# Transfers issued by SyncE stay in traced order through all eight batches of the first feed-forward, and the second feed-forward's preparation yields once more before its transposes

## The chip, the cores and the metric

The kernel runs on one core of a Trainium2 chip. The metric is the device time of one execution in microseconds (us). Before the change three runs took 2148.97, 2151.57 and 2152.36 us: the median is 2151.57. The engines are called by the profile's names: PE (TensorE matmuls), PEld (its weight loads), DVE (VectorE), ACT (ScalarE), POOL (GpSimd) and SP (SyncE, which here only issues transfers). A name with a q (SPq, ACTq) is the engine's own instruction queue as it issues transfers.

## The reference

x has 8 sequences of 512 tokens with 512 features. Two layers follow each other, and each adds two gated branches to x. Everything is float32.

```python
x = x + tanh(g_xattn[0]) * L0_xattn(layernorm(x), ctx)     # gated linear attention, 16 heads
x = x + tanh(g_ffn[0])   * L0_ffn(layernorm(x))            # 512 -> 2048, GELU, 2048 -> 512
x = x + tanh(g_xattn[1]) * L1_xattn(layernorm(x), ctx)     # softmax over 64 context rows
x = x + tanh(g_ffn[1])   * L1_ffn(layernorm(x))            # routed experts

# L0_ffn
h = gelu(x @ proj1.T + proj1_bias);  out = h @ proj2.T + proj2_bias

# L1_ffn: 8 of 32 experts, each 512 -> 2*192 -> 512
probs = softmax(x @ gate_weight.T);  top 8, normalised;  w_tg = sum of them by group
gu, dn = gate_up_proj[dominant_experts], down_proj[dominant_experts]
gate, up = split(x @ gu);  out = sum over g of w_tg * ((silu(gate) * up) @ dn)
```

## The kernel before

**Stages.** The work goes by batch (one sequence) through three stages: "xa0" (the first attention) for all eight batches, then "ff0" (the first feed-forward), then "ff1" (second attention and routed feed-forward together). In `work_list` the entries 0 to 7 are xa0, 8 to 15 are ff0 and 16 to 23 are ff1, so `n` in the main loop (L1365) is 8 to 15 in the first feed-forward and 16 to 23 in the second. Between stages x lies in DRAM: `load_x` (L142) brings a batch's 1 MB in on SP, `store_x` (L162) sends it out on ACT's queue (L170) after ff0, and on SP to the output after ff1.

**Products.** Every product is done by a scheme with seven half-size products (`ORDER`, L703) in place of eight. One step of the main loop is one of the seven: for an up product 8 matmuls with 128 x 256 outputs (L752), for ff0's down product 32 (L868), for ff1's down product 42 (L939), where the scheme is applied twice. The results are gathered in a few PSUM banks and combined by ACT copies (L764) and DVE additions (L807, L884). An ff0 batch has 35 steps (the first 33), an ff1 batch 49 or 50. The last two (or one) products of a unit are put behind the first of the next unit (`steps`, L1121), so a batch's x is complete at its successor's third step. Its store is traced at step 6 (`flush`, L1395).

**Weights.** They stream from DRAM through a ring of 16 tiles of 256 KB (`RING`, L129). After each step as many loads are traced as the step has freed tiles (L1379): one for an up product, four for an ff0 down product. So loads run 16 tiles ahead. They are issued on SP (L1292, L1300).

**The builder.** The weight combinations of the second feed-forward are made while the first one runs: `build_weights("ff1", ...)` (L347) loads raw expert weights on SP (L329, L340), combines them on POOL (`combining`, L232, and L388) and stores them in DRAM on SP (L366, L391). It is a generator, advanced once every fourth step (`next(builder)`, L1399). Its two buffers (`buildp`) take turns, so a load waits for the stores of the chunk before the last one. For each of the six up chunks one advance traces the next chunk's load and the first combination, three trace the others, and one traces seven stores of 256 KB. For each of the three down chunks one traces the load, eight trace a POOL operation each, and one traces seven stores of 448 KB. Its 61 advances fit in the eight batches.

**Preparation.** While batch n runs, batch n+1 is prepared by a generator (`prep_ff0`, `prep_ff1`) that the main loop advances now and then: `steps_of` (L1360) says how many advances there are and L1415 spreads them evenly over the batch's steps less six. `prep_ff1` first does the cross attention (`cross_attention`, L552), then `normed(..., "ff1_b")` (L395), the router, and the shares of the routed groups, which go to DRAM and come back spread over partitions (`spread_share`, L687, on SP). In `normed` DVE takes the statistics of x's four token tiles (L404, L405), adds epsilon (L409), POOL raises to the power -1/2 (L411), DVE normalises a tile (L418, `norm`), TensorE transposes it (L425) and ACT copies the transpose out (L428; both in `turn`). For the ff1 call there is one yield between the statistics and the first `norm` and `turn` (L412). x for batch n+2 is loaded at step 20 (L1404).

**Order.** The tile framework schedules the traced instructions: it may move an instruction ahead of others on its engine when its own model says that it is ready sooner. The wrapper `Ordered` (L47) gives an instruction an edge to the one traced before it on its engine, so that it stays behind everything traced earlier there. It does so for the engines that are in the set `in_order` at that moment. Such an instruction shows the wrapper's line, L60, in the profile, and a freely scheduled one its own line. During the attention stage the set holds "sync" and, in places, others. At L1341 it is reduced to "sync". In the main loop it is cleared at the start of every batch after the first of ff0, and `cross_attention` clears it too, after it has kept one DVE copy in order:

```python
        if n != at:
            if n > B:
                in_order.clear()
```

Of the kernel before, what the change touches and what calls it, by code (L numbers as in the profile page):

```python
# [31 lines left out]
B, S, D = 8, 512, 512  # L32
# [36 lines left out]
def flamingo_kernel(  # L69
# [23 lines left out]
    in_order = {"tensor", "vector", "scalar", "gpsimd", "sync"}  # L93
# [15 lines left out]
    def psum(name):  # L109
        return bank["ps"].tile([P, 512], F32, tag="ps", name=name)  # L110
# [284 lines left out]
    def normed(ph, b, tag):  # L395

        xb = xs[ph, b]
        xnT = work.tile([P, NC, S], F32, tag="xnT", name=f"xnT_{tag}")
        mv = small.tile([P, NT, 2], F32, tag="mv", name=f"mv_{tag}")
        if ph == "xa0":  # L400
            in_order.add("vector")
        for t in range(NT):
            st = small.tile([P, 6], F32, tag="st", name=f"st_{tag}_{t}")
            nc.vector.bn_stats(st, xb[:, t, :])  # L404
            nc.vector.bn_aggr(mv[:, t, :], st)  # L405
        if b:
            in_order.discard("vector")
        var = small.tile([P, NT], F32, tag="var", name=f"var_{tag}")
        nc.vector.tensor_scalar(var, mv[:, :, 1], LN_EPS, None, ALU.add)  # L409
        rstd = small.tile([P, NT], F32, tag="rstd", name=f"rstd_{tag}")  # L410
        nc.gpsimd.tensor_tensor(rstd, var, neg_half, ALU.pow)  # L411
        if ph == "xa0" or tag.startswith("ff1") or tag == "ff0_0":  # L412
            yield
        xn = {}

        def norm(t):
            xn[t] = work.tile([P, D], F32, tag="xn", name=f"xn_{tag}_{t}")
            nc.vector.tensor_scalar(  # L418
                xn[t], xb[:, t, :], mv[:, t, 0:1], rstd[:, t : t + 1], ALU.subtract, ALU.mult
            )  # L420

        def turn(t):
            pt = psum(f"pt_{tag}_{t}").rearrange("p (c q) -> p c q", q=P)
            for c in range(NC):
                nc.tensor.transpose(pt[:, c, :], xn[t][:, ts(c, P)], ident)  # L425

            at = t % 2 * 2 + t // 2 if tag.startswith("ff1") else t
            nc.scalar.copy(xnT[:, :, ts(at, P)], pt)  # L428

        if ph == "xa0" and b == 0:  # L430
            norm(0)
            norm(1)
            yield
            for t in range(NT):
                turn(t)
                if t + 2 < NT:
                    norm(t + 2)
                yield
            return xnT
        for t in range(NT):  # L440
            norm(t)
            turn(t)
            yield
        return xnT
# [82 lines left out]
    def prep_xa0(b):  # L527
        xnT = yield from normed("xa0", b, f"xa0_{b}")
        yield "last"
        blocks["xa0", b] = xnT, token_combinations("xa0", b, xnT)  # L530
# [12 lines left out]
    def prep_ff0(b):  # L543
        xnT = yield from normed("ff0", b, f"ff0_{b}")

        xb = xs["ff0", b]
        for t in range(NT):
            nc.gpsimd.tensor_tensor(xb[:, t, :], xb[:, t, :], b2_sb, ALU.add)  # L548
        yield "last"
        blocks["ff0", b] = xnT, token_combinations("ff0", b, xnT)  # L550

    def cross_attention(b):  # L552

        xb = xs["ff1", b]
        c2 = hpool.tile([P, D], F32, tag="ctx", name=f"ctxd_{b}", bufs=2)
        for h in range(2):
            nc.gpsimd.dma_start(out=c2[ts(h, M), :], in_=ctx_in[ts(b, M), :])
        maskf = small.tile([P, M], F32, tag="maskf", name=f"maskf_{b}")
        in_order.add("vector")
        nc.vector.tensor_copy(maskf, mask_sb[:, ts(b, M)])  # L560
        in_order.clear()
        shift = small.tile([P, M], F32, tag="shift", name=f"shift_{b}")
        nc.vector.tensor_scalar(shift, maskf, 1.0, NEG, ALU.subtract, ALU.mult)
        gate = small.tile([P, 1], F32, tag="gate", name=f"gate_{b}")
        nc.vector.reduce_max(gate, maskf, AX.X)
        nc.vector.tensor_scalar(gate, gate, gate_xa1, None, ALU.mult)
        ctxT = hpool.tile([P, NC, M], F32, tag="ctxdT", name=f"ctxdT_{b}", bufs=2)
        nc.gpsimd.dma_start(out=ctxT, in_=turned[b])
        xnT = yield from normed("ff1", b, f"xa1_{b}")

        pst = psum(f"pst_{b}")[:, 0:H2]
        for c in range(NC):
            for r in range(2):
                nc.tensor.matmul(  # L576
                    pst[ts(r, M), :],
                    lhsT=ctxT[:, c, :],
                    rhs=xnT[:, c, :].rearrange("p (u r q) -> p r u q", u=2, r=2)[:, r],
                    start=c == 0,  # L580
                    stop=c == NC - 1,
                )
        scT = hpool.tile([P, H2], F32, tag="scT", name=f"scT_{b}", bufs=1)
        nc.scalar.copy(scT, pst)
        yield
        psc = psum(f"psc_{b}")[:, 0:H2]
        for u in range(2):
            nc.tensor.transpose(psc[:, ts(u, P)], scT[:, ts(u, P)], ident)
        psc = psc.rearrange("p (t m) -> p t m", m=M)
        sc = hpool.tile([P, NT, M], F32, tag="sc", name=f"sc_{b}", bufs=1)  # L590
        nc.vector.scalar_tensor_tensor(
            sc, psc, 1.0 / math.sqrt(D), maskf.unsqueeze(1).to_broadcast([P, NT, M]), ALU.mult, ALU.mult
        )
        nc.vector.tensor_tensor(sc, sc, shift.unsqueeze(1).to_broadcast([P, NT, M]), ALU.add)
        top = small.tile([P, NT], F32, tag="top", name=f"top_{b}")
        nc.vector.tensor_reduce(top, sc, AX.X, ALU.max, negate=True)
        yield
        total = small.tile([P, NT], F32, tag="total", name=f"total_{b}")
        for t in range(NT):
            nc.scalar.activation(  # L600
                sc[:, t, :], sc[:, t, :], AF.Exp, bias=top[:, t : t + 1], accum_out=total[:, t : t + 1]
            )
        coef = small.tile([P, NT], F32, tag="coef", name=f"coef_{b}")
        nc.vector.reciprocal(coef, total)
        nc.vector.tensor_scalar(coef, coef, gate, None, ALU.mult)
        yield
        pe = psum(f"pe_{b}")[:, 0 : 2 * P].rearrange("p (u q) -> p u q", q=P)
        for u in range(NT // 2):
            nc.tensor.transpose(
                pe[:, u, :], sc[:, ts(u, 2), :].rearrange("p t m -> p (t m)"), ident  # L610
            )
        eT = hpool.tile([P, NT // 2, P], F32, tag="eT", name=f"eT_{b}", bufs=1)
        nc.scalar.copy(eT, pe)
        yield
        for t in range(NT):
            pr = psum(f"pr_{b}_{t}")
            half = ts(t % 2, M)
            nc.tensor.matmul(pr, lhsT=eT[half, t // 2, :], rhs=c2[half, :], start=True, stop=True)  # L618
            nc.vector.scalar_tensor_tensor(
                xb[:, t, :], pr, coef[:, t : t + 1], xb[:, t, :], ALU.mult, ALU.add  # L620
            )
            if t % 2:
                yield

    def prep_ff1(b):
        yield from cross_attention(b)
        xnT = yield from normed("ff1", b, f"ff1_{b}")

# [374 lines left out]
    class QUp(Up):  # L1003
        ph, i = "xa0", 0
# [354 lines left out]

    def steps_of(ph, b, _):  # L1360

        return 5 if ph == "ff0" else 21 if b else 23

    at, held = None, False
    for u, m, n in plan:  # L1365
        if n != at:
            if n > B:
                in_order.clear()
            if at is not None and n < 3 * B:
                for _ in work_list[n][2]:  # L1370
                    pass
            at, k, held = n, 0, False
# [39 lines left out]

        until = sum(p == n for _, _, p in plan) - 6
        count = steps_of(*work_list[n + 1])
        if k * count // until > (k - 1) * count // until:  # L1415
            held = next(prep, None) == "last"
# [47 lines left out]
```

## Time and profile before

The profiled execution took 2147.87 us, with a span of 2146.1 us from its first to its last instruction, and a mean granted TensorE clock of 0.995 of full speed. The table takes stretches of the span that lie inside the stages (all times in us; the busy time of PE counts matmuls).

| stretch | what runs | length | PE busy | DVE busy | POOL busy | DMA share | clock |
|---|---|---|---|---|---|---|---|
| 0 to 50 | loads, keys and values | 50.00 | 41.71 | 16.06 | 14.10 | 0.78 | 0.93 |
| 200 to 250 | first attention | 50.00 | 50.00 | 40.96 | 11.54 | 0.51 | 1.00 |
| 401.9 to 501.3 | first feed-forward, batch one | 99.40 | 99.40 | 32.18 | 34.14 | 0.95 | 1.00 |
| 501.3 to 601.5 | batch two | 100.20 | 98.63 | 33.15 | 38.09 | 0.77 | 1.00 |
| 601.5 to 717.3 | batch three | 115.80 | 101.20 | 34.26 | 20.58 | 0.71 | 0.96 |
| 717.3 to 815.8 | batch four | 98.50 | 98.50 | 30.24 | 6.05 | 0.54 | 1.00 |
| 1111.8 to 1220 | batch eight, prepares ff1 | 108.20 | 107.49 | 42.41 | 7.52 | 0.55 | 1.00 |
| 1650 to 1700 | second feed-forward | 50.00 | 49.98 | 39.80 | 0.00 | 0.89 | 1.00 |

A line of the timeline has the start, the duration, the engine, the source line, the operation, what it writes and reads, the shape and the count. In brackets at the end stands how long the engine was idle before it and what ended that idle time: "[11.40 <-ACT u_ff L764]" says that it stood 11.40 us until ACT's instruction at L764 that writes u_ff was done. A transfer's duration on SPq or ACTq is that of its issue, not of the transfer.

### The profile page before, as it was taken

The numbers are of one execution on the slowest core, as the hardware profiler recorded it, in microseconds if no ns is written. First come the engines' busy times: TensorE is split into PE (matmuls) and PEld (weight loads), VectorE is DVE, ScalarE is ACT, GpSimd is POOL, SyncE is SP. The second block draws the span as 40 slices with busy tenths as digits, with TensorE's granted clock in tenths as the row PEclk, the third lists the DMA queues.
The fourth block names the chain that finished last, engine by engine and source line by source line (L and its number), as shares of the span: only waits on it lengthen the run. The fifth ranks groups of instructions, "written<-read, shape, count | busy, mean of one in ns | idle before, by whom it ended". The sixth has DMA issues, their size and how long they took to land.

```text
span 2146.1 us, 30885 instructions
## 1 busy us (share of the span) xinstructions
PE 2094.4 (98%) x11452; PEld 1807.5 (84%) x11452; DVE 1242.7 (58%) x2289; ACT 557.0 (26%) x1146; POOL 251.0 (12%) x228
## 2 busy tenths in 40 slices
PE   8999999999979999999999999999999999999998
PEld 4778887788868888888888889898988989898988
DVE  3687787533323323232426278777767777776857
ACT  3433332212112213030314131222222221312121
POOL 3131111332340001010001000000001010000000
PEclk9999999999999999999999999999999999999999
DMA  7345634799686555555555558677676858585865
GB/s 224 116 153 176 201 109 125 222 316 333 209 260 206 188 151 187 153 186 172 167 184 158 192 168 270 199 247 221 213 247 191 271 164 287 161 282 161 268 202 165
DMA packets 258453, 434.84 MB, mean 203 GB/s; under 512 B 34304, under 2 KB 75936, under 8 KB 254208
## 3 DMA queue, kind: packets, MB, share of 16 engines
q1 hardware_dynamic: 250864, 406.10, 60.0%
q10 hardware_dynamic: 5856, 23.20, 3.0%
q0 software_dynamic: 1584, 3.57, 0.6%
q8 instruction: 92, 1.51, 0.3%
q14 instruction: 57, 0.47, 0.1%
HBM read 369.00 MB, written 63.77 MB: 202 GB/s over the span
## 4 chain that ended last, share of the span: by engine, by line
PE 79%; issue 8%; DVE 6%; DMA 4%; POOL 2%; SPq 1%; ACT 1%; ACTq 0%; POOLq 0%; DVEq 0%
PE x_ff L752 24%; PE w_ff L752 12%; PE x_ff_down L868 10%; PE z_ff L752 6%; PE x_ff_down L939 5%; PE w_ff_down L868 5%; PE w_ff_down L939 3%; PE z_ff_down L868 3%; PE z_ff_down L939 2%; PE v_ff_down L939 2%; PE pt_ff L425 1%; PE pt_xa L425 1%; PE pr L618 1%; PE pst L576 1%; DMA x_ff<-x_ff 1%
## 5 line engine op out<-in xcount | busy, mean ns | idle before, releaser
L764 ACT COPY u_ff<-x_ff 128x512 f32<-128x512 f32 x240 | 140.0, 584 | 758.5 <-PE x_ff L752 728.9
L752 PE MATMUL x_ff<-S_ff,w_ff_up 128*128 128x256 f32 x1280 | 306.1, 382 | 14.8 <-ACT u_ff L764 14.8
L752 PE MATMUL w_ff<-S_ff,w_ff_up 128*128 128x256 f32 x1280 | 304.5, 380 | 0.6 <-DVE a_ff L807 0.6
L752 PE MATMUL x_ff<-xnT_ff,w_ff_up 128*128 128x256 f32 x1280 | 296.8, 380 | 0.8 <-ACT u_ff L764 0.8
L752 PEld LDWEIGHTS x_ff<-S_ff,w_ff_up 128*128 128x128 f32 x1280 | 239.7, 191 | 53.4 <-ACT u_ff L764 15.8
L752 PEld LDWEIGHTS x_ff<-xnT_ff,w_ff_up 128*128 128x128 f32 x1280 | 238.9, 190 | 38.1 <-ACT u_ff L764 6.0
L752 PEld LDWEIGHTS w_ff<-S_ff,w_ff_up 128*128 128x128 f32 x1280 | 240.6, 190 | 35.5 <-issue 3.1
L868 PE MATMUL x_ff_down<-w_ff_down,a_ff 128*128 128x256 f32 x768 | 169.7, 379 | 0.0
L868 PEld LDWEIGHTS x_ff_down<-w_ff_down,a_ff 128*128 128x128 f32 x768 | 145.8, 190 | 19.8
L884 DVE SCALAR_TENSOR_TENSOR x_ff<-x_ff_down,gates,x_ff 128x512 f32<-128x512 f32 x32 | 24.0, 751 | 234.4 <-PE x_ff_down L868 234.4
L752 PE MATMUL z_ff<-xnT_ff,w_ff_up 128*128 128x256 f32 x640 | 151.7, 379 | 0.0
L752 PEld LDWEIGHTS z_ff<-xnT_ff,w_ff_up 128*128 128x128 f32 x640 | 119.7, 190 | 15.3
L868 PE MATMUL w_ff_down<-w_ff_down,s_ff 128*128 128x256 f32 x512 | 113.1, 379 | 0.0
L807 DVE TENSOR_TENSOR a_ff<-w_ff,u_ff 128x512 f32<-128x512 f32 x64 | 43.8, 684 | 115.7 <-ACT u_ff L764 113.6
L868 PEld LDWEIGHTS w_ff_down<-w_ff_down,s_ff 128*128 128x128 f32 x512 | 97.2, 190 | 13.2
L548 POOL TENSOR_TENSOR x_ff<-x_ff,b_sb 128x512 f32<-128x512 f32 x28 | 36.3, 1300 | 394.9 <-DVE xn_ff L418 351.6
L812 ACT ACTIVATE a_ff<-a_ff,b_sb 128x256 f32<-128x256 f32 x128 | 58.1, 500 | 92.2 <-DVE a_ff L807 92.2
L845 DVE TENSOR_TENSOR up_ff<-w_ff,u_ff 128x512 f32<-128x512 f32 x96 | 65.5, 683 | 27.9 <-ACT u_ff L764 27.9
L791 DVE TENSOR_TENSOR s_ff<-a_ff,a_ff 128x512 f32<-128x512 f32 x56 | 40.2, 718 | 58.1 <-ACT a_ff L812 57.9
L939 PE MATMUL x_ff_down<-w_ff_down,split_ff_down 128*128 128x128 f32 x576 | 70.1, 276 | 0.2
L939 PEld LDWEIGHTS x_ff_down<-w_ff_down,split_ff_down 128*128 128x128 f32 x576 | 66.8, 192 | 1.5 <-issue 1.5
L837 DVE TENSOR_TENSOR g_ff<-g_ff,share 128x512 f32<-128x512 f32 x96 | 65.9, 686 | 2.1
(260 smaller groups left out, 3246.5 us busy)
## 6 DMA issues: line engine op xcount, KB each, us to landing
w_ff_up<-ff_up SPq DMA_DIRECT2D x560, 256.0 KB
w_ff_down<-stream SPq DMA_DIRECT2D x288, 256.0 KB
w_ff_down<-ff_down SPq DMA_DIRECT2D x224, 256.0 KB
x_ff<-x_ff SPq DMA_DIRECT2D x16, 1024.0 KB
share<-shares SPq DMA_DIRECT2D x64, 256.0 KB
ff_up<-build_ff_up SPq DMA_DIRECT2D x42, 256.0 KB
spread<-over SPq DMA_DIRECT2D x32, 256.0 KB
x_ff<-x_xa ACTq DMA_DIRECT2D x8, 1024.0 KB
```

The source lines that it names most:

```text
L425: nc.tensor.transpose(pt[:, c, :], xn[t][:, ts(c, P)], ident)
L548: nc.gpsimd.tensor_tensor(xb[:, t, :], xb[:, t, :], b2_sb, ALU.add)
L752: nc.tensor.matmul(p[:, n, :], lhsT=w[:, c, ts(n, P)], rhs=moving, **self.mark(m, 2 * n + c),)
L764: nc.scalar.copy(self.s[m], p)
L791: nc.vector.tensor_tensor(s1, a21, a22, ALU.add)
L807: nc.vector.tensor_tensor(h, p, s, ALU.add)
L812: nc.scalar.activation(h[:, n, :], p[:, n, :], AF.Gelu, bias=b1_sb[:, f : f + 1])
L837: nc.vector.tensor_tensor(g, g, share, ALU.mult)
L845: nc.vector.tensor_tensor(u, p, s, ALU.add)
L868: nc.tensor.matmul(p[:, t, :], lhsT=a[:, k, ts(t, P)], rhs=w[k // 2][:, k % 2, :], **self.mark(m, 2 * k + t),)
L884: nc.vector.scalar_tensor_tensor(dst, src, GATE[self.ph], dst, ALU.mult, ALU.add)
L939: nc.tensor.matmul(p[n // 4][:, n % 4, :], lhsT=operand[k][:, c, :], rhs=w[at // 4][:, ts(at % 4, P)], start=m in self.OPENS and n % 4 == ...
```

## The change

Three things are edited. The set `in_order` is cleared once, at the start of the second feed-forward (n equal to 2 * B, 16), and no longer at each batch from the second of ff0 on. `cross_attention`, which runs for the first time in the last ff0 batch, takes only "vector" out of the set, where it cleared it. So "sync" stays in the set, and every transfer that SP issues keeps its traced place, through all eight batches of ff0. And `normed` yields twice instead of once between the statistics and the first normalisation when its tag begins with "ff1"; `steps_of` counts one advance more for `prep_ff1`.

```diff
@@ -411,6 +411,8 @@
         nc.gpsimd.tensor_tensor(rstd, var, neg_half, ALU.pow)
         if ph == "xa0" or tag.startswith("ff1") or tag == "ff0_0":
             yield
+        if tag.startswith("ff1"):
+            yield
         xn = {}
 
         def norm(t):
@@ -558,7 +560,7 @@
         maskf = small.tile([P, M], F32, tag="maskf", name=f"maskf_{b}")
         in_order.add("vector")
         nc.vector.tensor_copy(maskf, mask_sb[:, ts(b, M)])
-        in_order.clear()
+        in_order.discard("vector")
         shift = small.tile([P, M], F32, tag="shift", name=f"shift_{b}")
@@ -1359,12 +1361,12 @@
 
     def steps_of(ph, b, _):
 
-        return 5 if ph == "ff0" else 21 if b else 23
+        return 5 if ph == "ff0" else 22 if b else 24
 
     at, held = None, False
     for u, m, n in plan:
         if n != at:
-            if n > B:
+            if n == 2 * B:
                 in_order.clear()
             if at is not None and n < 3 * B:
                 for _ in work_list[n][2]:
```

## The prediction

> **What bounds the kernel now.** I read the page's busy shares first, then the busy time by stretches of one feed-forward batch each, then the waits of TensorE one by one, and at last the timeline around each wait.
>
> ```profile
> PE 2094.4 (98%) x11452; PEld 1807.5 (84%) x11452; DVE 1242.7 (58%) x2289; ACT 557.0 (26%) x1146; POOL 251.0 (12%) x228
> ```
>
> TensorE is busy 98% of the span, so only what leaves it idle or slows it can be won. The stretches below run from the first matmul of one batch's down product to that of the next (columns: stretch, its length, busy time and count by engine, granted clock, DMA share, GB/s). The first three are batches of the first feed-forward, the last two of the second.
>
> ```profile
> 446.89:547.17 100.28, 98.71 (x465) 86.60 (x465) 32.95 (x55) 22.63 (x48) 32.76 (x26) 1.00 0.92 309
> 547.17:662.94 115.77, 101.17 (x466) 87.67 (x465) 35.98 (x49) 22.30 (x48) 44.90 (x28) 0.96 0.78 249
> 662.94:761.39 98.45, 98.45 (x465) 86.68 (x465) 30.23 (x49) 22.79 (x48) 6.05 (x5) 1.00 0.54 171
> ...
> 1413.16:1529.93 116.77, 115.85 (x727) 102.43 (x726) 88.80 (x180) 29.16 (x63) 7.32 (x9) 1.00 0.73 226
> ...
> 1880.20:1995.85 115.65, 115.63 (x727) 102.51 (x726) 85.72 (x170) 29.07 (x63) 4.41 (x5) 1.00 0.68 216
> ```
>
> The same 465 matmuls take 98.45 us when nothing disturbs them, and 100.28 and 115.77 while POOL is busy building the second feed-forward's weights. In the second feed-forward a batch takes 116.77, and 115.65 where TensorE never waits. These differences are all that the change can win. The timeline of the worst stretch says where it goes:
>
> ```profile
> 600.74 0.75 DVE L884 SCALAR_TENSOR_TENSOR x_ff<-w_ff_down,gates,x_ff 128x512 f32<-128x512 f32 x1 [6.16 <-PE w_ff_down L868]
> 605.45 0.53 SPq L391 DMA_DIRECT2D stream<-build_ff_split  x1
> 616.71 0.33 ACTq L170 DMA_DIRECT2D x_ff<-x_ff  x1
> 617.07 0.59 ACT L764 COPY u_ff<-x_ff 128x512 f32<-128x512 f32 x1 [29.51 <-DMA build_ff_down<-in_dn]
> 617.71 3.64 PE L752 MATMUL x_ff<-S_ff,w_ff_up 128*128 128x256 f32 x8 [11.40 <-ACT u_ff L764]
> 622.54 0.37 SPq L153 DMA_DIRECT2D x_ff<-x_ff  x1
> 629.92 1.29 DVE L404 BATCH_NORM_STATS2 st_ff<-x_ff 128x6 f32<-128x512 f32 x2 [7.21 <-DMA x_ff<-x_ff]
> 634.00 1.99 PE L752 MATMUL x_ff<-S_ff,w_ff_up 128*128 128x256 f32 x8 [1.84 <-ACT u_ff L764]
> ```
>
> The batch's x is complete at 601.49, but its store, issued by ACT (L170), goes out only at 616.71. The releaser named is a load of the builder on SP, with which it shares no data, and that load was late because the builder's stores ahead of it on SP (L391) wait for POOL's results. Behind the store on ACT sits the eviction L764, and behind that TensorE, 11.40 us. The late store makes the next x load late (622.54), whose statistics hold DVE for 7.21 us, and TensorE loses 1.84 more, then 0.80 and 0.56. A wait of 6.95 us for x at 516.05 cost 1.57 in the batch before. All these transfers bear their own line numbers, so they were placed freely; those kept in order bear L60, the wrapper's line.
>
> **Part one, order on SP.** No instruction is added or removed. The edges that hold batch one's SP transfers in traced order now cover batches two to eight. The builder has 61 advances, one every fourth step, eight a batch; traced in order they fill the eight batches (the last store of the stream comes in the eighth batch, step 20), whereas before all its stores were out by 649.55. Three chunks' stream stores move from 550 to 650 us into batches six, seven and eight.
>
> The gain: (100.28 - 98.45) + (115.77 - 98.45) = 1.83 + 17.32 = 19.15 us. Of this 1.57 + 14.60 is idle TensorE and 2.98 its slower work after the idle time (granted clock 0.96 in that stretch). With the builder's traffic thinned out and traced at steps 4, 8 and so on, what SP issues just ahead of each x store is weight loads, as in the undisturbed batches, where the store at 717.33 leaves 0.08 us after its data (DVE, 716.50 and 0.75). I take all of it; the other end is nothing.
>
> What is queued where. A builder load needs the buffer whose stores were issued one advance earlier, four up steps of 1.73 us = 6.9 us. For the stream that is 7 x 448 KB = 3.21 MB; at 309 GB/s (the first stretch above) 10.4 us, and the 448 KB store at 605.45 took 4.93 us to land in the chain of waits, so SP may stand for 10.4 + 4.9 - 6.9 = 8.4 us, in batch six at step 8 and batch seven at step 16. Behind it stand weight loads. The ring holds 16 tiles, at 1.73 us a tile 27.6 us of work, less some 7.5 us for a load to land (x at 508.52 took 7.51): 20 us of cover. Cost nothing; without the cover 2 x 8.4 = 17 us.
>
> [...]
>
> The x load for two batches on now keeps its place at step 20. Batch one did so already, at 95% DMA share:
>
> ```profile
> 437.13 0.48 SPq L60 DMA_DIRECT2D x_ff<-x_ff  x1
> ...
> 444.43 1.29 DVE L404 BATCH_NORM_STATS2 st_ff<-x_ff 128x6 f32<-128x512 f32 x2 [2.00 <-DMA x_ff<-x_ff]
> ```
>
> DVE stood 2.00 us and TensorE not at all; 3.47 us at 728.63 cost nothing either, 6.95 cost 1.57, 7.21 cost 1.84. In batch three the builder stores 1.8 MB and in batch eight 3.2 MB right ahead of this load, at the same step. I charge two waits like the nearest rows, 1.57 and 1.84: +3.4 us. The low end is 0; the high end is a wait as long as the 15.3 us worked out above, of which 15.3 - 5.4 (6.95 less 1.57, what DVE can spare) = 9.9 us would reach TensorE, twice: +20.
>
> POOL's work is the same 48 operations, spread out. While they ran (400 to 720) the DVE's L791, L792 and L793 averaged 835, 802 and 878 ns, against 688, 689 and 682 later: 12 x (147 + 113 + 196) = 5.5 us, on an engine busy a third of the time. That moves and does not grow: 0.
>
> In the eighth batch two shares of the next stage's routing are spread by SP in order at step 29, behind ACT's store of wT (issued 1167.32). At worst SP stands from about 1162 to 1170, within the 20 us of cover: 0.
>
> **Part two, the further yield.** It adds no instruction either. With 22 advances in 43 or 44 steps in place of 21, the statistics come a step earlier and the turnings a step later (worked out from the loop: 22, then 26, 28, 30, 32, where it was 23, then 25, 27, 29, 31). What they meet now:
>
> ```profile
> 1497.41 0.17 DVE L409 TENSOR_SCALAR var_ff<-mv_ff 128x4 f32<-128x4 f32 x1
> 1497.66 1.03 POOL L411 TENSOR_TENSOR rstd_ff<-var_ff,neg_half 128x4 f32<-128x4 f32 x1 [5.39 <-DVE var_ff L409]
> 1498.73 1.00 DVE L418 TENSOR_SCALAR xn_ff<-x_ff,mv_ff,rstd_ff 128x512 f32<-128x512 f32 x2 [0.56 <-POOL rstd_ff L411]
> 1499.33 0.66 PE L425 MATMUL pt_ff<-ident,xn_ff 128*128 128x128 f32 x4 [0.90 <-DVE xn_ff L418]
> ```
>
> The turning stands in TensorE's queue 0.9 us before its operand. One step is 1.73 us, more than that. The wait occurs five times (1382.56, 1499.33, 1616.10, 1732.87, 1849.61) and each disturbed batch is 116.77 - 115.65 = 1.12 us longer: -5.6 us. The preparation in the last first-stage batch (24 advances in 29 steps) keeps its two steps between statistics and first turning, so its 0.55 us stays. What is late next: the router's product moves from step 33 to 34, its result's transpose is traced a step later, and the shares' store with it. In the stretch of 1529.66 that transpose already came after the last up matmul, and SP issued the first spread 2.4 us after the store, with other loads between; no TensorE wait hangs on it. Low end -6.3 (the 0.55 and 0.16 of that eighth batch too), high end +6.3 (a new 0.9 in each of seven preparations). I take -5.6, nearest to the row of 115.65.
>
> **Sum.** -19.15 + 3.4 - 5.6 = -21.4 us. The profiled execution took 2147.87 (span 2146.10 and 1.77 around it), so 2126.5 for one like it; the runs shown have the median 2151.57, 3.7 us above, from 2148.97 to 2152.36. From the median: 2130.2.
>
> **Rivals.**
> A, the forecast: 2130, own range 2125 to 2137. Chance 0.60.
> B, part one works but the stall comes back once, in batch eight, where 3.2 MB of stores, x and routing shares share SP. For it: the high end above. Against: 20 us of cover. Price as the stall of before, 17.3: 2151.57 - 19.15 + 17.3 - 5.6 = 2144. Chance 0.11.
> C, part two only moves the wait: the freely scheduled TensorE queue meets another late operand, for instance the router's chain, which ended 0.2 us late at 1165.28. Then 2151.57 - 19.15 + 3.4 = 2136. Chance 0.12.
> D, slower: the x load at step 20 lands so late in each of batches two to eight that DVE, with the statistics at its head, holds up the evictions. Each costs its wait less 5.4 us; seven of them outweigh 24.75 us of gains once the wait is over 5.4 + 24.75 / 7 = 8.9 us. At 11 us: 39.2 - 24.75 = +14.4, 2166. For it: 7.21 us has occurred. Against: 2.00 us in batch one under heavier traffic. Chance 0.11.
> E, it doesn't do what it says: the scheduler's free order was already the traced one where it matters, or the ACT store meets another SP transfer, and the stalls stay: 2152. Against: the stall's transfers bear free lines. Chance 0.06.
>
> **How the numbers follow.** What can't be told from no change is 0.2%, 4.3 us. A, B and C lie beyond it on the fast side: 0.60 + 0.11 + 0.12 = 0.83; E is the same, 0.06; D is slower, 0.11. The time is A's, 2130. The range starts at 2124, where the 3.4 us of late loads and the 0.7 us of the eighth batch fall away too and the runs' own scatter adds 2; it ends at 2148, past B and C, and leaves out E and D, 0.17, and a little below.
>
> **What would show it.** Right: the stretch of 115.77 falls to 98.5 to 100, the 29.51 us idle of ACT is gone, builder stores appear under L60 up to some 1120 us, and the 0.9 us waits at L425 go from the second feed-forward. Wrong: DVE waits for x over 5 us in several batches (D), TensorE waits for a weight tile (the cover was too small), or ACT waits again for a builder transfer (B, E).

## The result

Over 20 runs of each the changed kernel takes 2149.29 us (median; 2147.61 to 2152.63) and the kernel before 2151.10 (2148.13 to 2154.18). The ratio is 0.9994, with a 95% interval from 0.9987 to 1.0001: no difference that can be measured, where 2130 had been forecast. The profiled execution has a span of 2147.9 us at a mean granted clock of 0.992 (2146.1 and 0.995 before). One run of the first experiment below, 2423.9 us at a granted clock of 0.85, is left out of that experiment's ratio. TensorE's busy time is almost what it was, in the page's first part:

```profile
PE 2096.3 (98%) x11452; PEld 1810.3 (84%) x11452; DVE 1241.4 (58%) x2289; ACT 557.4 (26%) x1146; POOL 251.7 (12%) x228
```

The end has not moved, but the inside has. I cut the span at the first matmul of the down product of batch one and of batch eight in the first feed-forward (446.89 and 1165.55 before, 448.68 and 1151.15 after, as the view of the critical chain has them). Between the cuts the time falls from 718.66 to 702.47 us, by 16.19; behind them it grows from 980.55 to 996.75, by 16.20. So a gain was made and given back whole. The stretches of the changed kernel from one down product to the next show both (columns as before: length, busy time and count of PE, PEld, DVE, ACT and POOL, granted clock, DMA share, GB/s):

```profile
448.68:547.13 98.45, 98.45 (x465) 86.69 (x465) 31.18 (x51) 22.75 (x48) 16.57 (x14) 1.00 0.73 227
547.13:645.58 98.45, 98.45 (x465) 86.68 (x465) 31.29 (x45) 22.73 (x48) 11.21 (x8) 1.00 0.68 215
...
842.48:942.99 100.51, 98.72 (x465) 86.60 (x465) 29.48 (x47) 22.73 (x48) 17.72 (x12) 1.00 0.68 211
942.99:1042.28 99.29, 99.29 (x469) 87.42 (x469) 29.27 (x42) 23.34 (x49) 14.50 (x11) 1.00 0.67 205
...
1408.49:1528.61 120.12, 117.27 (x727) 103.56 (x726) 89.05 (x180) 29.06 (x62) 6.98 (x9) 0.99 0.70 221
...
1648.13:1766.25 118.12, 115.59 (x727) 102.42 (x726) 88.45 (x179) 29.05 (x62) 6.97 (x9) 1.00 0.71 222
```

The first two lines answer to the 100.28 and 115.77 of before: both are now 98.45 with TensorE never idle. The last two answer to the 116.77: a batch of the second feed-forward now takes 118.1 to 120.1. Where the 29.51 us of ACT's idle time stood, the timeline of the changed kernel has this:

```profile
600.69 0.75 DVE L886 SCALAR_TENSOR_TENSOR x_ff<-w_ff_down,gates,x_ff 128x512 f32<-128x512 f32 x1 [6.16 <-PE w_ff_down L870]
...
601.52 0.33 ACTq L170 DMA_DIRECT2D x_ff<-x_ff  x1
...
604.14 0.59 ACT L766 COPY u_ff<-x_ff 128x512 f32<-128x512 f32 x1 [16.63 <-PE x_ff L754]
```

The store leaves 0.08 us after its data (600.69 + 0.75 = 601.44), and the ACT copy behind it waits for nothing but its own operand from TensorE. So part one did what it was made for. Two short waits are left in batches six and seven, both beside the builder's late chunks, which now reach that far:

```profile
928.53 0.32 SPq L60 DMA_DIRECT2D x_ff<-x_ff  x1
...
936.98 0.69 DVE L404 BATCH_NORM_STATS2 st_ff<-x_ff 128x6 f32<-128x512 f32 x1 [7.18 <-DMA x_ff<-x_ff]
...
940.99 1.99 PE L754 MATMUL x_ff<-S_ff,w_ff_up 128*128 128x256 f32 x8 [1.79 <-ACT u_ff L766]
...
1046.37 2.07 POOL L388 TENSOR_TENSOR build_ff_split<-build_ff_down,build_ff_split 128x896 f32<-128x896 f32 x1
...
1048.40 1.02 POOL L411 TENSOR_TENSOR rstd_xa<-var_xa,neg_half 128x4 f32<-128x4 f32 x1
...
1050.65 1.99 PE L754 MATMUL w_ff<-S_ff,w_ff_up 128*128 128x256 f32 x8 [0.58 <-DVE a_ff L809]
```

In batch six the statistics start 8.45 us after the issue of x's load, and DVE stands 7.18 us for it. In batch seven the power for 1/rms stands on POOL behind the last of the builder's additions, 2.1 us after its operand (DVE, 1045.00 and 1.31). Together they cost TensorE 2.37 us. A third wait, 0.55 us before at the first turning of batch eight, is 0.9 us now. It is 0.9 in the first experiment too and 0.6 in the second, so it goes with the order.

What the second feed-forward lost is one wait per batch that was not there before. TensorE's waits from 1160 us on, in the view of waits (total, times, longest), are this line alone:

```profile
PE pw L677 <- DVE w L673: 15.5, 6, 2.8
```

`pw` is the transpose of the routed groups' shares, TensorE's last step in the router's chain. The five waits of 0.9 us for the turnings, 4.5 us in that view of the kernel before, are gone as forecast. The timeline of the changed kernel around the wait in the batch that ends at 1528 says why it is late:

```profile
1508.41 0.28 DVE L657 MAX8 best<-router 128x8 f32<-128x32 f32 x2
...
1511.60 0.55 DVE L928 TENSOR_TENSOR split_ff_down<-a_ff 128x384 f32<-128x384 f32 x1
...
1514.88 0.55 DVE L931 TENSOR_TENSOR split_ff_down<-a_ff,split_ff_down 128x384 f32<-128x384 f32 x1
...
1515.42 0.17 DVE L658 MATCH_REPLACE8 rest<-best,router 128x32 f32<-128x32 f32 x1
...
1523.78 0.42 DVE L673 TENSOR_REDUCE w<-wg_e 128x8 f32<-128x256 f32 x1 [0.90 <-POOL wg_e L670]
1524.26 0.40 PE L677 MATMUL pw<-ident,w 128*32 128x128 f32 x1 [2.83 <-DVE w L673]
```

And the same chain in the kernel before:

```profile
1520.20 0.37 DVE L655 MAX8 best<-router 128x8 f32<-128x32 f32 x2 [0.41 <-ACT router L650]
...
1527.71 0.55 DVE L926 TENSOR_TENSOR split_ff_down<-a_ff 128x384 f32<-128x384 f32 x1
...
1528.88 0.42 DVE L671 TENSOR_REDUCE w<-wg_e 128x8 f32<-128x256 f32 x1 [0.62 <-POOL wg_e L668]
...
1529.66 0.27 PE L675 MATMUL pw<-ident,w 128*32 128x128 f32 x1
```

Before, the top-8 search went from its first MAX8 to the normalised shares (L661, at 1521.84) in 1.6 us, and the eight additions that combine the down product's operand (`combine(2)` and `combine(4)`, `split_ff_down`) came afterwards, the first among the reductions to `w` and the others behind the last of them. After, the search is cut in two: between its first MAX8 and its MATCH_REPLACE stand five gate and up operations and all eight additions, from 1508.61 to 1515.35, 6.7 us. The code says where the new order comes from. One more yield moves every later piece of the preparation by one advance. The search moved from step 37 to step 38 of its batch, and at step 38 (`m == 2`, which comes second in a unit's `ORDER` of 1, 2, 6, 5, 7, 4, 3; here it is the last up product's) the main loop traces `combine(2)` and `combine(4)` before it advances the preparation. The additions are now traced ahead of the search, and DVE takes them first. TensorE's transpose waits 2.53 to 2.83 us in six batches.

### The profile page after: what moved, and what is told of

The parts are those of the page before. It is cut to its first block, busy times and chain, and to the rows that moved or that the text cites. A ratio compares the mean times of both kernels' runs of the same rounds, so it can differ in the third digit from the quotient of the medians.

```text
span 2147.9 us, 30849 instructions
## 1 busy us (share of the span) xinstructions
PE 2096.3 (98%) x11452; PEld 1810.3 (84%) x11452; DVE 1241.4 (58%) x2289; ACT 557.4 (26%) x1146; POOL 251.7 (12%) x228
## 4 chain that ended last, share of the span: by engine, by line
PE 77%; issue 7%; DVE 7%; DMA 4%; POOL 3%; SPq 1%; ACT 1%; POOLq 0%; ACTq 0%; DVEq 0%
PE x_ff L754 24%; PE w_ff L754 12%; PE x_ff_down L870 10%; PE z_ff L754 6%; PE x_ff_down L941 5%; PE w_ff_down L870 5%; PE w_ff_down L941 3%; PE z_ff_down L870 3%; PE v_ff_down L941 2%; PE pt_ff L427 1%; SPq L60 1%; PE pt_xa L427 1%; POOL wg_e L670 1%; PE pr L620 1%; PE pst L578 1%
## 5 line engine op out<-in xcount | busy, mean ns | idle before, releaser
L754 PEld LDWEIGHTS z_ff<-xnT_ff,w_ff_up 128*128 128x128 f32 x640 | 119.4, 190 | 15.5 <-DMA w_ff_up<-ff_up 0.4
L837 DVE SCALAR_TENSOR_TENSOR g_ff<-th_ff,x_ff 128x512 f32<-128x512 f32 x48 | 32.9, 686 | 73.9 <-ACT th_ff L836 73.9
```

Source lines behind the costliest of these rows:

```text
L754: nc.tensor.matmul(p[:, n, :], lhsT=w[:, c, ts(n, P)], rhs=moving, **self.mark(m, 2 * n + c),)
L837: nc.vector.scalar_tensor_tensor(g, th, 1.0, p, ALU.add, ALU.mult)
```

## The experiments

Each kernel's times stand against runs of the kernel before on the same chip, and its profile is cut at the same two places. The cuts are read to 0.1 us here, and from the timeline, where a matmul starts some 0.2 us earlier than in the chain (all in us; the first part is what lies ahead of batch one's first down matmul). Ahead of the first cut all but the fourth, seventh and eighth run the same code, and among the others it still lies between 446.7 and 449.0: so much a single profile scatters. In the kernel with x loaded earlier the records of four matmuls at the first cut are missing.

| kernel | median | ratio, 95% interval | span | first cut | between the cuts | behind |
|---|---|---|---|---|---|---|
| before | 2151.1 | | 2146.1 | 446.7 | 718.7 | 980.7 |
| after | 2149.29 | 0.9994 [0.9987, 1.0001] | 2147.9 | 448.5 | 702.5 | 996.9 |
| 1 order alone | 2132.55 | 0.9920 [0.9905, 0.9936] | 2129.8 | 447.1 | 702.0 | 980.7 |
| 2 yield alone | 2169.28 | 1.0092 [1.0076, 1.0107] | 2162.1 | 448.6 | 718.0 | 995.5 |
| 3 after, combined later | 2129.4 | 0.9903 [0.9888, 0.9918] | 2129.1 | 449.0 | 701.9 | 978.2 |
| 4 order, fast builder | 2139.53 | 0.9953 [0.9938, 0.9968] | 2137.1 | 447.9 | 708.5 | 980.7 |
| 5 order, combined earlier | 2137.0 | 0.9939 [0.9924, 0.9954] | 2135.3 | 448.3 | 702.3 | 984.7 |
| 6 last yield merged | 2130.69 | 0.9909 [0.9894, 0.9925] | 2129.1 | 448.6 | 701.7 | 978.8 |
| 7 as 3, x earlier | 2141.67 | 0.9960 [0.9946, 0.9973] | 2139.9 | - | - | 978.1 |
| 8 as 6, POOL in order | 2135.58 | 0.9935 [0.9922, 0.9949] | 2134.9 | 448.7 | 707.5 | 978.7 |

**1. The order of the transfers alone.** The yield is taken out again.

```diff
-        if tag.startswith("ff1"):
-            yield
-        return 5 if ph == "ff0" else 22 if b else 24
+        return 5 if ph == "ff0" else 21 if b else 23
```

> Only the SP order of the change, with the single yield of before. Router theory (the further yield moved the router's chain behind other DVE work, and TensorE waits for it 2.5 us in six batches) and step theory (the chain is late merely because it starts a step later) both expect the whole second stage as before: first stage 16 us shorter, 2151.1 - 16.2 = 2135, no wait of TensorE at pw over 0.3 us. SP theory (the kept order itself delays the second stage): about 2150, the pw waits stay.

2132.55 us: 18 faster than before. The part behind the cuts is that of before to 0.1 us, and the view of waits from 1160 us on has the old waits and no wait for `pw`:

```profile
PE pt_ff L425 <- DVE xn_ff L418: 4.5, 5, 0.9
```

The whole gain of the first stage is the order of SP's transfers, and the whole loss of the second belongs to the yield.

**2. The yield alone.** The order is that of before, the yield and the counts those of after.

```diff
-        in_order.discard("vector")
+        in_order.clear()
-            if n == 2 * B:
+            if n > B:
                 in_order.clear()
```

> Only the further yield, SP as before. Router and step theories: the stall of 11.4 us at the third batch stays and six pw waits of about 2.5 us come, 2151.1 + 16.2 = 2167. SP theory: 2151 or a little less, no pw waits.

2169.28 us: 18 slower than before (20 by the ratio). The stall of the first stage is back, in its timeline with the same releaser as before:

```profile
618.22 0.33 ACTq L170 DMA_DIRECT2D x_ff<-x_ff  x1
...
618.58 0.59 ACT L766 COPY u_ff<-x_ff 128x512 f32<-128x512 f32 x1 [30.81 <-DMA build_ff_down<-in_dn]
...
619.22 3.35 PE L754 MATMUL x_ff<-S_ff,w_ff_up 128*128 128x256 f32 x7 [12.70 <-ACT u_ff L766]
```

And TensorE waits 15.7 us for `pw`. The two parts add up to within 1.4 us: against before they shift the stretch between the cuts by -16.7 and -0.7 (after: -16.2) and the part behind them by 0 and +14.8 (after: +16.2). The profile here is that of the shortest of the four runs, 2163.89 us.

**3. The combinations two steps later.** The kernel after, with `combine(2)` and `combine(4)` traced behind the search instead of ahead of it. Nothing else is moved; in `ORDER` the product 5 comes two steps after the product 2.

```diff
-            if m == 2:
+            if m == 5:
                 down_of[u.b].combine(2)
                 down_of[u.b].combine(4)
```

> The changed kernel, with the two combinations for the down product (eight DVE operations of 0.55 us) traced two steps later, behind the router's top-8 in traced order. Router theory: the chain gets its place on DVE back, the pw waits shrink from 2.5 us to under 1, and the time falls to 2128 to 2136. Step theory: the waits stay, 2149.

2129.4 us, and the waits for `pw` are 0.23 to 0.25 us. Its timeline in the same batch:

```profile
1506.05 0.28 DVE L657 MAX8 best<-router 128x8 f32<-128x32 f32 x2
...
1509.31 0.18 DVE L658 MATCH_REPLACE8 rest<-best,router 128x32 f32<-128x32 f32 x1
...
1509.76 0.54 DVE L928 TENSOR_TENSOR split_ff_down<-a_ff 128x384 f32<-128x384 f32 x1
...
1517.97 0.42 DVE L673 TENSOR_REDUCE w<-wg_e 128x8 f32<-128x256 f32 x1 [0.61 <-POOL wg_e L670]
...
1518.44 0.28 PE L677 MATMUL pw<-ident,w 128*32 128x128 f32 x1 [0.23 <-DVE w L673]
```

The five gate and up operations still stand inside the search (3.3 us from its MAX8 to its MATCH_REPLACE, against 7.0 in the kernel after), but the additions start behind it, among its later pieces. The yield is there, the step is the later one, and the 15.5 us are gone: the additions' place in DVE's queue made the wait, not the later step as such. This is also what the change would have brought with that collision avoided: some 21 us by the ratio, near the -21.4 of the forecast. The parts are not those of the forecast, though: behind the cuts the gain is 2.5 us, not 5.6.

**4. Order with a faster builder.** The order alone, and the builder advanced every second step, so that its traffic is nearer to that of the kernel before: the last store of its stream is out at 750.2 us, against 649.55 before and 1144.65 after.

```diff
-        if k % 4 == 0:
+        if k % 2 == 0:
```

> As e1, but the builder is advanced every second step, so that its work is done in four batches instead of eight. If the gain of the first stage comes from keeping transfers from being overtaken: as e1 within 4 us, ACT never waits over 5 us for a builder transfer. If it comes from spreading the builder's work thin: a stall of 5 to 17 us comes back in batches two to four, 2140 to 2152.

2139.53 us, 7 above the first where the first theory allowed 4. No copy of ACT waits for a builder transfer, so the order takes that stall away even with the builder advanced twice as often; at the full density of the kernel before it was not tried. But a smaller loss of another kind appears in its timeline:

```profile
645.38 1.27 POOL L235 TENSOR_TENSOR build_ff_down<-build_ff_down 128x512 f32<-128x512 f32 x1 [27.04 <-DMA build_ff_down<-in_dn]
...
657.23 2.08 POOL L388 TENSOR_TENSOR build_ff_split<-build_ff_down,build_ff_split 128x896 f32<-128x896 f32 x1
659.27 1.02 POOL L411 TENSOR_TENSOR rstd_ff<-var_ff,neg_half 128x4 f32<-128x4 f32 x1
660.32 1.00 DVE L418 TENSOR_SCALAR xn_ff<-x_ff,mv_ff,rstd_ff 128x512 f32<-128x512 f32 x2 [5.30 <-POOL rstd_ff L411]
...
665.85 2.50 PE L868 MATMUL z_ff_down<-w_ff_down,a_ff 128*128 128x256 f32 x5 [5.40 <-ACT a_ff L812]
```

A late builder load makes POOL start eight operations late, the small power for the norm queues behind them, and DVE, ACT and TensorE follow, 5.40 us. So the thinner traffic too has a share in the gain: the 7 us between this kernel and the first.

**5. The combinations a step earlier.** The order alone, with the single yield, but `combine(2)` and `combine(4)` traced at step 37 in place of 38 (`m == 3`, the last product of the last but one up unit), ahead of the search at its old place.

```diff
+        if isinstance(u, Ff1Up) and u.i == FF1_UNITS[-2] and m == 3:
+            down_of[u.b].combine(2)
+            down_of[u.b].combine(4)
...
-            if m == 2:
-                down_of[u.b].combine(2)
-                down_of[u.b].combine(4)
```

> As e1, with the single yield, but the two combinations for the down product are traced one step earlier than before, ahead of the router's top-8 in traced order. In DVE's queue the eight combinations then stand ahead of the last two of the router's four reductions to w. Router theory: pw waits 1.5 to 3 us in six batches without any further yield, 2132.6 + 9 to 20 = 2142 to 2152. Step theory: nothing was moved later in the router's chain, so as e1, 2133.

2137.0 us, between what the two theories gave. It is slower than the order alone by some 4 us, the direction that the router theory asked for, but `pw` waits only 0.34 to 0.54 us, less than expected. As the expectation had it, the additions did not come ahead of the search but behind the second reduction to `w`, 0.25 us after the last of their operands (`a_ff`, L849, 1511.45 and 0.68):

```profile
1512.38 0.55 DVE L926 TENSOR_TENSOR split_ff_down<-a_ff 128x384 f32<-128x384 f32 x1
...
1515.66 0.55 DVE L929 TENSOR_TENSOR split_ff_down<-a_ff,split_ff_down 128x384 f32<-128x384 f32 x1
...
1516.83 0.42 DVE L671 TENSOR_REDUCE w<-wg_e 128x8 f32<-128x256 f32 x1 [0.62 <-POOL wg_e L668]
```

Only the last two of the four reductions to `w` stood behind them. Here the edit of the traced order moved the additions only as far as their operands allowed.

**6. The further yield without the later step.** The kernel after, but with no yield behind the last turning, so that what follows the turnings, the search too, keeps its step.

```diff
-            yield
+            if t + 1 < NT or not tag.startswith("ff1"):
+                yield
...
-        return 5 if ph == "ff0" else 22 if b else 24
+        return 5 if ph == "ff0" else 21 if b else 23
```

> SP order, the further yield before the turnings, but no yield after the last turning, so that the router's product, and all behind it, keeps its old step (21 advances as before). Router theory: DVE's order at the combinations is that of e1, so pw waits at most 0.3 us and the waits of 0.9 us at the turnings go as well: 2132.6 - 5 = 2127. Step theory, in the form that the router needs as many steps after the turnings as before: its product now stands right behind the last turning, and TensorE waits 0.5 to 2 us for its copy in each batch, 2133 to 2140.

2130.69 us, the same as the third within their intervals. Behind 1160 us the view of waits has no line for TensorE at all, and the same batch of the second feed-forward is filled to 0.02 us:

```profile
1406.02:1522.19 116.17, 116.15 (x725) 102.66 (x724) 89.09 (x180) 29.07 (x62) 7.06 (x9) 1.00 0.75 227
```

So the further yield takes the five waits away without bringing those for `pw`. It is not free, and 2127 had been expected. The router's product now stands right behind the last turning, and TensorE runs 6 of its 32 matmuls (L635, 1498.37), then two of an up product's, then the other 26. From its start to that of the next up product, at 1501.74, it takes 3.37 us, against 2.84 in the kernel before (1514.62 to 1517.46). That is 0.53 us in each of seven batches, the 3.7 us above 2127. Whether this kernel beats the order alone is not settled by the runs, as their intervals overlap; behind the cuts its profile is 1.9 us shorter.

**7. x loaded earlier.** The third kernel, with the load of x seven steps earlier, aimed at the two waits left in batches six and seven.

```diff
-        if k == 20 and n + 2 < 3 * B:
+        if k == 13 and n + 2 < 3 * B:
```

> As e3, with the x load traced at step 13 instead of 20. If the two remaining waits of the first stage (1.04 and 0.75 us at 940.68 and 1050.51, batches six and seven) come from x landing behind the builder's transfers, they shrink and batches six and seven fall from 99.7 and 99.5 towards 98.45: 2127. If they come from GpSimd, where the builder's operations stand ahead of the power for the statistics, they stay: 2129.

2141.67 us, a miss: 12 us slower than the third. In batch six:

```profile
932.82 1.29 DVE L404 BATCH_NORM_STATS2 st_ff<-x_ff 128x6 f32<-128x512 f32 x2 [7.79 <-DMA x_ff<-x_ff]
...
939.01 1.02 POOL L411 TENSOR_TENSOR rstd_ff<-var_ff,neg_half 128x4 f32<-128x4 f32 x1
...
941.27 3.78 PE L754 MATMUL w_ff<-S_ff,w_ff_up 128*128 128x256 f32 x8 [7.90 <-DVE a_ff L809]
```

The statistics start 4.2 us earlier than in the kernel after, but they stand earlier in DVE's queue. DVE waits 7.79 us for x, then 3.14 us more for the power, which POOL makes behind the builder's operations (norm, L420, at 940.07). The additions that TensorE needs stand behind both, and it waits 7.90 us.

**8. POOL in order too.** The sixth kernel, with GpSimd's queue kept in traced order through the first feed-forward, so that the builder's later operations can't go ahead of a norm's power.

```diff
-    in_order &= {"sync"}
+    in_order &= {"sync", "gpsimd"}
```

> The kernel with the transfers' order and the further step, but nothing between the last turning and the end, now with GpSimd's queue too kept in the program's order through the first feed-forward. Theory that the two waits left in batches six and seven (0.98 and 0.98 us in that kernel) are the norms' 1/rms standing behind the builder's operations in GpSimd's queue: those two waits go, and the median falls by about 2 us, from 2130.7 to 2128 to 2129.5. Theory that they come from something else (the late load of x alone, or the statistics behind VectorE's own work): both waits stay within 0.3 us and the median stays at 2130 to 2131.5. Rival: GpSimd's order makes the norms wait for builder operations that themselves wait for a load, as in the kernel with the builder every second step; then a new wait of TensorE of 3 us or more shows in one batch and the median is above 2133.

2135.58 us, and the waits grew, to 1.44 us in batch six, 3.01 in batch seven and a new 1.79 in batch eight. In batch seven:

```profile
1045.08 0.62 DVE L409 TENSOR_SCALAR var_xa<-mv_xa 128x4 f32<-128x4 f32 x1
1045.61 1.11 POOL L60 DMA_DIRECT2D ctxd<-in_ctx  x2
...
1048.87 1.04 POOL L60 TENSOR_TENSOR rstd_xa<-var_xa,neg_half 128x4 f32<-128x4 f32 x1
1049.90 2.06 POOL L60 TENSOR_TENSOR build_ff_split<-build_ff_down 128x896 f32<-128x896 f32 x1
1049.94 2.30 DVE L420 TENSOR_SCALAR xn_xa<-x_ff,mv_xa,rstd_xa 128x512 f32<-128x512 f32 x1 [4.25 <-POOL rstd_xa L60]
```

The last builder operations do come after the power now, but the power stands behind six transfers that POOL issues, 3.3 us of them. That explains only part: the power is made 0.8 us later than in the sixth kernel (1048.08 there), the statistics start 2.4 us later (1042.13 against 1039.77), and the norm behind the power takes 2.30 us in place of 0.55 while POOL makes the builder's next addition. The size is that of the expectation's rival, the cause is another, and no run parts these three. In batch six TensorE's wait (940.82) ends before the power is even made (943.55), so the power is not its cause there. What would clear both waits, 2 us together, stays open.

## Why the prediction was wrong

**The step that failed** is the last one of part two, "What is late next". It said of the router's chain that it moves by a step and that "no TensorE wait hangs on it", and took -5.6 for the whole part. The part cost +16.2. The five waits of 0.9 went, as worked out; but six waits for `pw`, 15.5 us, came, and the matmuls behind four of them ran slower. Behind each of those waits the start of the next down product came 4.18, 4.12, 4.40 and 4.40 us after `pw`, against 2.71 in the two batches where nothing slowed down: 6.3 us. 15.5 + 6.3 - 5.6 = 16.2, the difference measured behind the cuts.

The row read there was 1529.66, where the transpose had no wait. What I checked was its place in TensorE's queue, behind the last up matmul. What I did not check is how much time was left ahead of it: the last reduction ended at 1528.88 + 0.42 = 1529.30, only 0.36 us before, and a step is 1.73 us. That alone did not make the loss. In the third kernel the chain is a step later too, and TensorE, which there takes `pw` behind the first down product, waits 0.23 to 0.25 us. What made it is that I did not list what DVE does in the step that the chain moved into. For SP the prediction did count what each moved transfer is moved past; for DVE it did not.

**Rival C** had the place and the mechanism, the router's chain late for TensorE, at a chance of 0.12. Its price was wrong: it let the new wait eat just the gain of part two. A wait that takes the place of another has no reason to be of its size, and each of these was three times as long as a wait that went.

**The size of part two** was off as well. With the collision out of the way the part behind the cuts is 2.5 us shorter than before in the third kernel and 1.9 in the sixth, not 5.6. The five waits go in both, but six waits of 0.23 to 0.25 us and slightly slower matmuls behind them (eight in 1.94 to 1.99 us, against 1.89 in the sixth) stay in the third, and the split router product costs 3.7 us in the sixth. That the third comes near -21.4 in all is partly luck, as part one gave more than forecast.

**Part one was right.** Forecast -19.15 + 3.4 = -15.75; measured between the cuts -16.19, and -17 by the ratio of the order alone (0.008 of 2151, its interval reaching from 14 to 20). The stretches fell to 98.45, the ACT wait went, the builder's stores run in order up to 1143, and no TensorE wait for a weight tile appeared (the view of waits between the cuts has 1.8, 0.9 and 0.6 us for ACT and DVE alone): the hold reckoned for SP cost nothing. The 3.4 us for late loads of x were 2.4, in batches six and seven in place of three and eight, and 0.58 of them came with the power queued on POOL on top of a late x. That the free order of SP's transfers makes the stall is shown by taking it away and bringing it back (ACT's wait for the builder's load is 29.51 us before, 30.81 in the second experiment, and not there in the first). That the store on ACT waited for that very load is the profile's reading; why a store on one queue should wait for a load on another was not tried.

**Rivals B, D and E** did not occur. No stall came back in batch eight; no wait for x held DVE over 7.18 us; and the order does what it says. The result is of E's size by another cause. The range, 2124 to 2148, reached past B and C; a part two that takes back all that part one brings was in none of the cases.

## What to carry to other kernels

When a yield, a step or a due time is moved, every later piece of that generator moves too: list, on each engine, what is traced in the step that each piece lands in, above all the last piece, and compare its end before with the moment its reader needs it. Here a step of 1.73 us with 0.36 us of room came out at 0.25 us of wait in the third kernel, and at 2.5 to 2.8 us where the step put eight additions, 3.75 us, into the chain. If the later pieces need not move, give the step back behind the part that wanted it, as the sixth kernel does, and look what then moves together; a change of two parts that comes out at nothing is worth taking apart, as one of them was worth 18 us alone.

## What the runs showed of the hardware

Four of the six waits for `pw` cost TensorE more than their length. After the 2.53 us that ended at 1763.38 the eight matmuls of the next product took their usual 1.89 us; after the 2.53 us that ended at 1881.72 they did not. The changed kernel's timeline:

```profile
1764.36 1.89 PE L754 MATMUL w_ff<-S_ff,w_ff_up 128*128 128x256 f32 x8
...
1883.13 3.15 PE L754 MATMUL w_ff<-S_ff,w_ff_up 128*128 128x256 f32 x8
```

Four of six waits between 2.53 and 2.83 us were followed by such a slowdown, at 1.4 to 1.7 us each, and the granted clock of their stretches is 0.99 against 1.00 in the two others; after the 1.79 us in batch six none is seen (its stretch has 1.00). The trace shows where equal waits part. The granted clock is at 0.50 for just 3.41 us after each of the four, from 1523.86, 1643.33, 1882.26 and 2001.73 on. These starts are 119.47, 238.93 and 119.47 us apart, which is 35, 70 and 35 times 3.413 us. In stretches laid on that grid (columns as in the result) it goes with how long TensorE was busy in the stretch before:

```profile
1639.92:1643.33 3.41, 1.40 (x9) 0.94 (x8) 0.84 (x2) 0.48 (x1) 2.16 (x3) 1.00 0.70 227
1643.33:1646.74 3.41, 2.89 (x8) 2.36 (x9) 0.55 (x2) 0.85 (x2) 0.01 (x1) 0.50 0.02 5
...
1759.38:1762.80 3.42, 1.47 (x10) 1.01 (x8) 0.84 (x2) 0.48 (x1) 2.10 (x3) 1.00 0.73 228
1762.80:1766.21 3.41, 2.83 (x15) 2.52 (x16) 1.40 (x3) 0.85 (x2) 0.07 (x1) 1.00 0.19 41
```

Ahead of the four slow stretches TensorE was busy 0.87 to 1.40 us of 3.41; the two waits without a slowdown fall across two stretches, and left it 1.47 us or more in each. Read the same way from 60 us on, no full-speed stretch in the traces before and after the change is followed by half the clock after more than 1.40 us of work, and none by the full clock after less than 1.47. What sets the granted clock no run shows.
